# Seven block products for the second feed-forward product, in the slots beside cross-attention

## The chip, the cores and the metric

The kernel runs on one core of one Trainium2 chip. The metric is the device time of one execution in microseconds (us); all data is float32. The engines are called by the names of the profile: PE (TensorE, matrix products), PEld (its weight loads), DVE (VectorE), ACT (ScalarE), POOL (GpSimd) and SP (the queue that issues most transfers here).

## What is computed

The input `x` has 8 batches of 256 tokens with 256 features. It passes through three residual stages, each followed by a layer norm:

```python
x = layernorm(x + attn(x))       # 4 layers: self-attention and an MLP 256 -> 1024 -> 256, exact gelu
x = layernorm(x + xattn(x, ctx)) # cross-attention to 120 context rows, 16 heads of 64
x = layernorm(x + ffn(x))        # W1, W2 composed from 32 low-rank terms each, tanh gelu
```

The last stage is `h = gelu(x @ W1); y = h @ W2` with W1 of 256x1024 and W2 of 1024x256. An MLP of the first stage has the same shapes, with biases. The cross-attention has a mask under which query i sees key j only where j = i (mod 256), so that each query attends to one key of its own or to none.

## The kernel before

All weights and the running `x` of each batch (`xs[b]`, two tiles of 128 tokens by 256 features) stay on the core. The program has no scheduler for PE, ACT, DVE and POOL: their instructions run in the order in which the source issues them (`manual_schedule`), and each engine works through its own queue in that order. SP's order is the framework's.

The 32 units of self-attention (4 layers x 8 batches) run in a first loop, each MLP four units behind its attention. A second loop (lines 1413 to 1460) has 16 slots, of which 11 have work:

- Slots 0 to 7 run the cross-attention of batch `s` (class `Cross`) beside a feed-forward `ff`.
- In slots 0, 1 and 2 `ff` is the last three MLPs of layer 3 (class `Mlp`, batches 5, 6, 7); in slots 3 to 10 it is the composed feed-forward of batches 0 to 7 (class `Composed`). So slots 8, 9 and 10 have a feed-forward alone.

Both feed-forwards are a `Seven`: the first product, transposed (`hT`, 1024 rows by 256 tokens), is a 2x2 by 2x2 block product done with seven block products instead of eight, in Winograd's form. Each block product (`one`, line 596) is four matmuls with 128 moving columns. Its operand sums are made on POOL: those of W1 once for each layer (`first_sums`, lines 560 to 563), those of the turned input for each batch (`turn_sums`, lines 574 to 577). The seven are issued in the groups `p16`, `p5`, `p27` and `p34`, with DVE and ACT adding partial sums between them:

- `p16`: blocks 1 and 6; ACT copies block 1, DVE adds it to block 6 in PSUM (line 614).
- `p5`: block 5; ACT copies the two partial sums (lines 620, 622).
- `p27`: block 2 ends h11, which ACT puts through gelu; block 7, added by DVE to h22 (line 628), then gelu.
- `p34`: block 3, added by DVE to h21 (line 633), then gelu; block 4 ends h12, then gelu.

So the four gelus run on ACT in the order h11, h22, h21, h12. An `Mlp` does each as four activations of 128 columns, with a bias (line 918); a `Composed` as one of 512 (line 960).

The second product before (`second`, line 645) is a plain one: for token tile i, eight matmuls with `hT` blocks as weights and 256 columns of W2 moving. `second(1)` reads h22 and h21, `second(0)` reads h11 and h12. In an MLP both fill one PSUM bank, and DVE adds it to `xs[b]` (line 233). In a composed feed-forward each tile has its own bank; DVE adds it (line 973), normalises that tile (`bn_stats`, lines 181 to 184; a power on POOL, line 189; a scaling on DVE, line 195) and SP writes 128 KB (line 976).

At the end of a slot before, PE's order is: block 4 of `ff`; `turn_o` (transposes of the cross-attention's values); `second(1)`; `nxt_m.turn` (four transposes of the next feed-forward's input, line 214) with `turn_sums` on POOL; `second(0)`; `x.out` (the output projection, lines 1176 to 1179, added by DVE at line 233); `nxt_x.turn` (two transposes, line 1079, then a copy on DVE and two bias additions on POOL, line 229). DVE centres the next batch (`nxt_x.centre`, line 195) between. The next slot begins with the cross-attention's `scores` (line 1090). In a slot `old.finish_moments` and `old.finish` normalise the previous cross-attention's batch on DVE, after `p16`.

The PSUM pool `bank_g`, from which all feed-forward banks come, has four banks.

Of the kernel before, what the change touches and what calls it, by code (L numbers as in the profile page):

```python
# [8 lines left out]
F32 = mybir.dt.float32  # L9
# [6 lines left out]
P = 128  # L16
# [5 lines left out]
def tile_decoder_postln(  # L22
# [29 lines left out]
    nc = tc.nc  # L52

    B, T, D = x.shape
    DEPTH = Wq.shape[0]
    WT = T // P
# [12 lines left out]
    NP, _, R = fc1_A.shape  # L69
# [4 lines left out]
    out_v = out.rearrange("b (w p) d -> p (b w) d", p=P)  # L74
# [8 lines left out]
    xs = [const.tile([P, WT, D], F32, name=f"x_{b}") for b in range(B)]  # L83

    def load_x(b, queue):
        queue.dma_start(out=xs[b], in_=x_v[:, b * WT : (b + 1) * WT, :])
# [16 lines left out]
    at = 0  # L103
    offs = {}
    for name, v in (("g1", ln1_g), ("b1", ln1_b), ("g2", ln2_g), ("b2", ln2_b), ("ff", b1)):
        n = v.shape[0] * v.shape[1] // P
# [18 lines left out]
    w2c = const.tile([P, NF, D], F32, name="w2c")  # L125
# [30 lines left out]
    mlp_ws = {}  # L156
# [5 lines left out]
    work = ctx.enter_context(tc.tile_pool(name="work", bufs=2))  # L162
# [8 lines left out]
    def bank_g(name):  # L171
        return ps_g.tile([P, 512], F32, tag="bank_g", name=name)
# [19 lines left out]
    def centre(dst, src, mv, rstd):  # L192

        for i in range(src.shape[1]):
            nc.vector.tensor_scalar(  # L195
                dst[:, i, :],
                src[:, i, :],
                mv[:, i, 0:1],
                rstd[:, i : i + 1],
                ALU.subtract,  # L200
                ALU.mult,
            )

    def normalise(dst, src, name, last=False):
        centre(dst, src, *moments(src, name, last))
# [447 lines left out]
                        between()  # L653


    class Attention:


# [286 lines left out]
    class Composed(Seven):  # L945
# [24 lines left out]
        def second(self, i):  # L970
            super().second(i)
            x, at = xs[self.b][:, i : i + 1, :], self.b * WT + i
            nc.vector.tensor_add(x[:, 0, :], x[:, 0, :], self.ps[:, i * D : (i + 1) * D])
            y = work.tile([P, 1, D], F32, tag="xnm", name=f"y_{self.name}_{i}")
            normalise(y, x, f"{self.name}_{i}", self.b == B - 1)
            nc.sync.dma_start(out=out_v[:, at : at + 1, :], in_=y)

# [3 lines left out]
    class Context:  # L983
# [29 lines left out]
        def take(self):  # L1013
            b0, ps = self.b0, self.ps
            nc.vector.tensor_copy(
                self.cT[:, :, b0 : b0 + 2, :],
                ps[:, : 2 * NC * S2].rearrange("p (c b j) -> p c b j", c=NC, b=2),
            )
# [39 lines left out]
    class Cross:  # L1058
# [128 lines left out]
        finish = centre  # L1187
# [17 lines left out]
    UNITS = DEPTH * B  # L1205
    compose = Compose()
    cross = None
# [20 lines left out]
        out=before,  # L1228
        in_=before,
# [49 lines left out]
    nxt_x = None  # L1279
    nxt_m = None  # L1280
    nxt_c = None
    mlp_sums = {}
    for s in range(1, UNITS + 1):
        ff = nxt_m
        after = Attention(s + 1) if s + 1 < UNITS else None
        nxt_m = Mlp(s + 1 - LAG) if s + 1 >= LAG else None
        filled = cross is None
        if after and filled and s > 1:
            after.moments()
        if new and s > 1:  # L1290
            new.qkv(nxt_c)
        nxt_c = None
        if filled:
            compose.combine(0)
            if compose.done():
                compose.last.final()
                comp_stack.close()
                cross = ctx.enter_context(tc.tile_pool(name="cross", bufs=1))
        if s == 1:
            compose.run()  # L1300
            after.moments()
        if not new:
            ff.turn()
            ff.turn_sums()
            old.totals()
            old.divide(range(HL))
        old.linear_sums()
        old.divide_c()
        if not new:
            ff.p16()  # L1310
        old.turn_p()
        if ff and new:
            ff.turn()
            ff.turn_sums()
            compose.combine(1)
        if new:
            new.scores()
        old.values()
        if not new:
            nxt_x = Cross(0, cx)  # L1320
            nxt_x.moments()
        if 2 < s + 2 < B:
            load_x(s + 2, nc.scalar)
        if s == 1:
            mlp_ws[0] = load_mlp(0, nc.scalar)
        if after and filled and not ff:
            after.centre()
        if s == 1:
            next(first[1])
            next(first[1])  # L1330
        if ff:
            if new:
                ff.p16()
            if after and filled:
                after.centre()
            elif after:
                after.moments()
            old.out(0)
            ff.p5()
            ff.p27()  # L1340
            old.out(1)
            ff.p34()
            compose.weigh()
        else:
            compose.run()
            old.out(0)
            old.out(1)
            if s == 1:
                for _ in range(3):
                    next(first[1])  # L1350
        if after and not filled:
            after.centre()
        if nxt_m:
            nxt_m.moments()
        if s == LAG - 2:
            mlp_sums[0] = first_sums(mlp_ws[0][0])
        if ff and ff.b == B - 1 and ff.l + 1 < DEPTH:
            mlp_sums[ff.l + 1] = first_sums(mlp_ws[ff.l + 1][0])
        turn_cx = cx and s < UNITS
        if turn_cx:  # L1360
            i = 2 * (s - (UNITS - B + LAG))
            cx.turn(i)
            cx.take()
        if new:
            new.exps()
            if not filled:
                new.head_exps((0, 1))

        vsums = None if new else cx.sums()
        if ff:  # L1370
            ff.second(1, vsums and (lambda: next(vsums)))
        if vsums:
            next(vsums)
        if after:
            after.turn()
        if new:
            new.head_exps((2, 3) if not filled else range(HL))
            new.softmax_q()
        if filled:
            compose.run()  # L1380
        if new and after:
            new.totals()
            new.divide(range(HL))
        if nxt_m and after and not filled:
            nxt_c = nxt_m.centre
        elif nxt_m:
            nxt_m.centre()
        if ff:
            ff.second(0)
        l, b = divmod(s + 1, B)  # L1390
        if b == B - 2 and l + 1 < DEPTH:
            attn_ws[l + 1] = load_attn(l + 1, nc.scalar)
        l, b = divmod(s + 1 - LAG, B)
        if l >= 0 and b == B - 2 and l + 1 < DEPTH:
            mlp_ws[l + 1] = load_mlp(l + 1, nc.scalar)
        if s == UNITS - B + LAG - 1:
            xwq = wpool.tile([P, NC, XI], F32, tag="w1", name="xwq")
            xwo = wpool.tile([P, NM, D], F32, tag="w2", name="xwo")
            cx = Context()
            nc.sync.dma_start(out=xwq, in_=xWq.rearrange("(c p) n -> p c n", p=P))  # L1400
            nc.sync.dma_start(out=xwo, in_=xWout.rearrange("(c p) n -> p c n", p=P))
        if turn_cx:
            cx.take_sums()
            if i == B // 2 - 2:
                cx.load(1)
        if s == UNITS:
            nxt_x.centre()
            cx.project()
        old, new = new, after
    nxt_x.turn()  # L1410
    nxt_m.turn()
    old = None
    for s in range(2 * B):
        x, ff = nxt_x, nxt_m
        nxt_x = Cross(s + 1, cx) if s + 1 < B else None
        u = UNITS - LAG + s + 2
        nxt_m = Mlp(u) if u < UNITS else Composed(u - UNITS) if u < UNITS + B else None
        if ff and s == 0:
            ff.turn_sums()
        if x:  # L1420
            x.scores()
        if ff:
            ff.p16()
        if old:
            old.finish_moments()
        if x:
            x.values(0)
        if old:
            old.finish()
        old = x  # L1430
        if ff:
            ff.p5()
            ff.p27()
        if nxt_x:
            nxt_x.moments()
        if x:
            x.values(1)
        if nxt_m:
            nxt_m.moments()
        if ff:  # L1440
            ff.p34()
        if nxt_m:
            nxt_m.centre()
        if u == UNITS:
            mlp_sums[DEPTH] = first_sums(w1c)
        if x:
            x.turn_o()
        if ff:
            ff.second(1)
        if nxt_m:  # L1450
            nxt_m.turn()
            nxt_m.turn_sums()
        if nxt_x:
            nxt_x.centre()
        if ff:
            ff.second(0)
        if x:
            x.out()
        if nxt_x:
            nxt_x.turn()  # L1460


# [56 lines left out]
```

## Time and profile before

| | us |
|---|---|
| median of three runs | 1214.65 (1214.35 to 1214.76) |
| the profiled execution, its time | 1214.1 |
| the profiled execution, its span | 1212.1 |
| start of slot 0 (first matmul of its scores) | 928.38 |
| start of slot 3 | 1017.00 |
| start of slot 8 | 1164.16 |
| start of the last `second` pair (slot 10) | 1200.07 |

The profile is of one execution. A line of the timeline has the start and the duration in us, the engine, the source line, the operation, what it writes and reads (the program's names), the shapes, and how many instructions were merged (x16); in brackets stands the idle time before it and what ended that. A line with several instructions gives the whole stretch. Matmuls are pipelined and their ends are modelled, so two neighbouring starts say more than a duration.

### The profile page before, as it was taken

The page shows a single profiled execution, that of the slowest core. Times are in us where ns is not written, and L with a number is a line of the kernel's source. Part 1 is how long each engine was busy: PE and PEld are TensorE (multiplying, and loading weights), DVE is VectorE, ACT ScalarE, POOL GpSimd, SP SyncE. Part 2 cuts the span into 40 slices and gives each one's busy share as a digit, 9 for nine tenths or more (in the row PEclk, how much of TensorE's full clock was granted, in tenths as well). Part 3 has the DMA queues.
Part 4 walks back from the last instruction along what each step waited for, and adds up shares of the span by engine and source line. Part 5 has one row for each costly group of instructions (what it writes and reads, how often), then busy time and mean ns, then how long its engine had stood idle before and what let it go on. Part 6 is the DMA issues. An engine that isn't in the chain of part 4 may idle for free.

```text
span 1212.1 us, 24094 instructions
## 1 busy us (share of the span) xinstructions
PE 1198.7 (99%) x9133; PEld 960.7 (79%) x9133; DVE 852.5 (70%) x2422; ACT 636.8 (53%) x1774; POOL 440.0 (36%) x663
## 2 busy tenths in 40 slices
PE   8999999999999999999999999999999999999998
PEld 5556789888888888878888888888787777777787
DVE  6878788777878777677877777777874455555543
ACT  4444555655444567766677666776563333323223
POOL 6665455555565322222422222242232223222220
PEclk9999999999999999999999999999999999999999
DMA  5633131101310120020001002021000000000000
GB/s 161 211 89 113 44 92 45 40 24 30 115 45 1 29 98 2 1 65 12 1 1 41 1 2 75 2 70 26 10 11 9 1 9 10 18 18 9 10 14 23
DMA packets 29505, 47.81 MB, mean 39 GB/s; under 512 B 3150, under 2 KB 22734, under 8 KB 29134
## 3 DMA queue, kind: packets, MB, share of 16 engines
q0 software_dynamic: 6656, 20.98, 5.9%
q10 hardware_dynamic: 13024, 14.07, 3.6%
q1 hardware_dynamic: 9710, 11.23, 2.9%
q8 instruction: 72, 1.18, 0.4%
q14 instruction: 43, 0.35, 0.1%
HBM read 44.17 MB, written 2.10 MB: 38 GB/s over the span
## 4 chain that ended last, share of the span: by engine, by line
PE 96%; DVE 3%; ACT 1%; issue 0%; POOL 0%; POOLq 0%; ACTq 0%; DVEq 0%
PE ps_p_m L645 18%; PE qkv_a L713 9%; PE ps_h_m_u L596 7%; PE ps_h_m_a L596 5%; PE ps_h_m_d L596 5%; PE ps_p_a L239 5%; PE ps_w L387 5%; PE ps_qk_a L693 4%; PE ps_w L449 4%; PE ps_p_f L645 4%; PE ps_pT_a L860 3%; PE sc_a L744 2%; PE ps_y_c L1179 2%; PE ps_xq_c L1090 2%; PE ps_xk_c L1090 2%; PE ps_xv_c L1090 2%
## 5 line engine op out<-in xcount | busy, mean ns | idle before, releaser
L645 PE MATMUL ps_p_m<-w,h_m 128*128 128x256 f32 x1024 | 233.5, 380 | 0.0
L645 PEld LDWEIGHTS ps_p_m<-w,h_m 128*128 128x128 f32 x1024 | 189.4, 191 | 22.8 <-ACT h_m L918 0.3
L229 POOL TENSOR_TENSOR x<-x,b 128x256 f32<-128x256 f32 x64 | 48.3, 774 | 226.2 <-DVE xn_m L195 226.2
L713 PE MATMUL qkv_a<-wa,xT_a 128*128 128x512 f32 x256 | 115.1, 592 | 0.0
L775 ACT ACTIVATE p_a<-sc_a,nm_a 128x128 f32<-128x128 f32 (+1 forms) x256 | 103.6, 430 | 2.2 <-DVE nm_a L757 2.0
L713 PEld LDWEIGHTS qkv_a<-wa,xT_a 128*128 128x128 f32 x256 | 48.7, 190 | 47.5 <-issue 45.8
L757 DVE TENSOR_REDUCE nm_a<-sc_a 128x1 f32<-128x128 f32 (+1 forms) x256 | 79.5, 352 | 4.4
L918 ACT ACTIVATE h_m<-h_m,cols 128x128 f32<-128x128 f32 x256 | 78.6, 405 | 6.2 <-DVE h_m L633 5.5
L229 POOL TENSOR_TENSOR x<-x,bo 128x256 f32<-128x256 f32 x64 | 48.1, 771 | 73.3 <-DVE xn_a L195 73.2
L596 PE MATMUL ps_h_m_a<-xT_m,w 128*128 128x128 f32 x512 | 70.6, 281 | 0.5 <-DVE xT_m L223 0.5
L300 POOL DMA_INDIRECT ga<-in_L_ffn_fc_A_dram,idx_a x64 | 62.2, 972 | 23.6 <-issue 15.3
L720 ACT COPY v<-qkv_a 128x256 f32<-128x256 f32 x64 | 23.8, 372 | 84.5 <-PE qkv_a L713 84.5
L596 PE MATMUL ps_h_m_u<-tx_m,w 128*128 128x128 f32 x512 | 67.8, 276 | 0.0
L596 PEld LDWEIGHTS ps_h_m_a<-xT_m,w 128*128 128x128 f32 x512 | 62.4, 192 | 4.8 <-issue 1.5
L239 PE MATMUL ps_p_a<-wo,oT_a 128*128 128x256 f32 x256 | 65.7, 381 | 0.0
L805 DVE TENSOR_TENSOR p_a<-p_a,psum_a 128x384 f32<-128x384 f32 x128 | 63.8, 560 | 1.1
L596 PEld LDWEIGHTS ps_h_m_u<-tx_m,w 128*128 128x128 f32 x512 | 62.3, 192 | 0.0
L693 PE MATMUL ps_qk_a<-xT_a,wa 128*128 128x256 f32 x256 | 60.7, 380 | 0.9 <-ACT aw L354 0.9
L645 PE MATMUL ps_p_f<-w2c,h_f 128*128 128x256 f32 x256 | 57.8, 380 | 0.0
L387 PE MATMUL ps_w<-gbt,at 128*128 128x512 f32 x128 | 56.7, 596 | 0.0
L753 DVE TENSOR_TENSOR sc_a<-sc_a,causal 128x256 f32<-128x256 f32 x128 | 54.3, 424 | 3.4 <-PE sc_a L744 2.2
L775 ACT ACTIVATION_READ_ACCUMULATOR p_a<-sc_a,nm_a 128x1 f32 x256 | 55.8, 218 | 0.0
(269 smaller groups left out, 2704.0 us busy)
## 6 DMA issues: line engine op xcount, KB each, us to landing
w<-in_L_attn_W_dram ACTq DMA_DIRECT2D x8, 1024.0 KB, 6.3
xwkv<-in_L_xattn_Wkv_dram SPq DMA_DIRECT2D x1, 2048.0 KB, 9.1
x_c<-in_x_dram SPq DMA_DIRECT2D x8, 256.0 KB, 2.6
out_dram<-y_f SPq DMA_DIRECT2D x16, 128.0 KB, 1.7
x<-in_x_dram ACTq DMA_DIRECT2D x6, 256.0 KB, 3.4
ga<-in_L_ffn_fc_A_dram,idx_a POOLq DMA_INDIRECT x64, 3.4
xwq<-in_L_xattn_Wq_dram SPq DMA_DIRECT2D x1, 1024.0 KB, 5.1
xwo<-in_L_xattn_Wout_dram SPq DMA_DIRECT2D x1, 1024.0 KB
```

What stands on the lines that cost most here:

```text
L229: nc.gpsimd.tensor_add(xb[:, i, :], xb[:, i, :], bias)
L239: nc.tensor.matmul(ps[:, i * D : (i + 1) * D], lhs(c, i), w[:, c, :], start=c == 0, stop=c == n_in - 1,)
L387: nc.tensor.matmul(ps, self.at[k][:, m * P : (m + 1) * P], self.b[k][:, n * 512 : (n + 1) * 512], start=k == 0, stop=k == PG - 1,)
L596: nc.tensor.matmul(ps[:, f * P : (f + 1) * P], self.ws[n][:, f * P : (f + 1) * P], self.rhs[n], start=start and f == 0, stop=stop and f == ...
L645: nc.tensor.matmul(self.ps[:, i * D : (i + 1) * D], self.h[k][:, f, :], self.w2[:, half * 4 + f, :], start=k in (11, 22) and f == 0, stop= ...
L693: nc.tensor.matmul(ps[s], wa[:, c, s * HW : (s + 1) * HW], xT[:, c, :], start=c == 0, stop=c == NC - 1,)
L713: nc.tensor.matmul(t, xT[:, c, w * P : (w + 1) * P], wa[:, c, 2 * HW :], start=c == 0, stop=c == NC - 1,)
L757: nc.vector.tensor_reduce(self.nmax[:, h, w : w + 1], sc[:, s], AX.X, ALU.max, negate=True)
L775: nc.scalar.activation(flat[:, s], sc[:, s], AF.Exp, bias=self.nmax[:, h, w : w + 1], accum_out=self.psum[:, h, w : w + 1],)
L805: nc.vector.tensor_tensor(p, p, self.psum[:, h, :, None].to_broadcast([P, 3, P]), ALU.mult)
L918: nc.scalar.activation(dst[:, f, :], src[:, f * P : (f + 1) * P], AF.Gelu, bias=col("ff", i))
L1090: nc.tensor.matmul(ps[:S2], lhs(c), w[:, c, off : off + 512], start=c == 0, stop=c == NC - 1)
```

## The change

In the eight slots with cross-attention the second product is done with seven block products too, and the end of the slot has a new order. Slots 8 to 10 keep the old form.

New functions (in `Seven`, and `w2_sums` beside it):

```diff
+        def two(self, n, ps, slot, a, start=False):
+            for f in range(4):
+                nc.tensor.matmul(
+                    ps[:, slot * P : (slot + 1) * P],
+                    a[:, f, :],
+                    self.w2s[n][:, f, :],
+                    start=start and f == 0,
+                    stop=f == 3,
+                    skip_group_check=True,
+                )
+        def take(self, blocks, src):
+            x = xs[self.b].rearrange("p i (n d) -> p (i n) d", n=2)[:, blocks, :]
+            nc.vector.tensor_add(x, x, src)
+        def second_plain(self):
+            h = self.h
+            self.ps = bank_g(f"ps_p_{self.name}")
+            self.two(1, self.ps, 0, h[11], start=True)
+            self.two(4, self.ps, 2, h[22])
+            self.two(2, self.ps, 1, h[12])
+        def h_sums(self):
+            h = self.h
+            s1, s2 = (cross.tile([P, 4, P], F32, tag=f"h{i}", name=f"h{i}_{self.name}") for i in (1, 2))
+            nc.gpsimd.tensor_add(s1, h[21], h[22])
+            nc.gpsimd.tensor_sub(s2, s1, h[11])
+            nc.gpsimd.tensor_sub(h[21], h[11], h[21])
+            nc.gpsimd.tensor_sub(h[22], h[12], s2)
+            self.hs = {5: s1, 6: s2, 7: h[21], 3: h[22]}
+        def second_early(self):
+            ps = self.ps.rearrange("p (k d) -> p k d", k=4)
+            self.take(slice(0, 1), ps[:, 0:1, :])
+            self.take(slice(0, 3, 2), ps[:, 1:3, :])
+        def second_sums(self):
+            ps, hs = self.ps, self.hs
+            pd = bank_g(f"ps_pd_{self.name}")
+            self.two(6, ps, 0, hs[6])
+            self.take(slice(1, 2), ps[:, None, :P])
+            self.two(5, pd, 0, hs[5], start=True)
+            self.take(slice(3, 4), pd[:, None, :P])
+            self.two(7, ps, 0, hs[7])
+            self.take(slice(2, 4), ps[:, None, :P].to_broadcast([P, 2, P]))
+            self.two(3, pd, 0, hs[3])
+            self.take(slice(1, 2), pd[:, None, :P])
+    def w2_sums(w2):
...
+        nc.gpsimd.tensor_sub(t1, b[0][1], b[0][0])
+        nc.gpsimd.tensor_sub(t2, b[1][1], t1)
+        nc.gpsimd.tensor_sub(t3, b[1][1], b[0][1])
+        nc.gpsimd.tensor_sub(t4, b[1][0], t2)
```

`two` is one block product: four matmuls with 128 moving columns. Blocks 1, 4 and 2 use plain blocks of h (with sums of W2 only in block 4); blocks 6, 5, 7 and 3 use sums of h, which POOL makes in `h_sums`. Blocks 6 and 7 add up in the PSUM columns that hold block 1, and `take` adds the columns to the 128x128 blocks of `xs[b]` that they belong to. `w2_sums` makes the sums of W2: once before slot 0 for the MLP's, and once at the end of slot 2 for the composed W2.

The end of a slot and the composed feed-forward's last step:

```diff
         if s == UNITS:
             nxt_x.centre()
             cx.project()
+            w2s = w2_sums(mlp_ws[DEPTH - 1][1])
...
         if x:
             x.turn_o()
-        if ff:
-            ff.second(1)
-        if nxt_m:
+            ff.w2s = w2s
+            ff.second_plain()
+            ff.h_sums()
             nxt_m.turn()
             nxt_m.turn_sums()
-        if nxt_x:
-            nxt_x.centre()
-        if ff:
+            ff.second_early()
+            if nxt_x:
+                nxt_x.centre()
+            x.out()
+            if nxt_x:
+                nxt_x.turn()
+            ff.second_sums()
+            if u == UNITS:
+                w2s = w2_sums(w2c)
+            if u > UNITS:
+                ff.finish()
+        elif ff:
+            ff.second(1)
+            if nxt_m:
+                nxt_m.turn()
+                nxt_m.turn_sums()
             ff.second(0)
-        if x:
-            x.out()
-        if nxt_x:
-            nxt_x.turn()
...
+        def finish(self):
+            at = self.b * WT
+            y = work.tile([P, WT, D], F32, tag="xnm", name=f"y_{self.name}")
+            normalise(y, xs[self.b], self.name)
+            nc.sync.dma_start(out=out_v[:, at : at + WT, :], in_=y)
```

PE's order at the end of a slot becomes: `turn_o`; blocks 1, 4, 2; the next feed-forward's transposes; `x.out`; the next cross-attention's transposes; blocks 6, 5, 7, 3. On DVE the order is: the copy of `nxt_m.turn`, two takes, `nxt_x.centre`, `x.out`'s addition, the copy of `nxt_x.turn`, four takes, and in slots 3 to 7 `finish`, which normalises both tiles of the batch at once. On POOL `h_sums` stands ahead of `turn_sums`, and the composed `w2_sums` behind the bias additions of slot 2. Two output writes of 128 KB become one of 256 KB in each of the slots 3 to 7.

More of the change, by code (lines that the diff above doesn't have):

```diff
@@ new lines, in w2_sums @@
+    def w2_sums(w2):
+        b = [[w2[:, 4 * k : 4 * k + 4, n * P : (n + 1) * P] for n in range(2)] for k in range(2)]
+        t1, t2, t3, t4 = (cross.tile([P, 4, P], F32, tag=f"t{i}", name=f"t{i}") for i in range(1, 5))
+        nc.gpsimd.tensor_sub(t1, b[0][1], b[0][0])
+        nc.gpsimd.tensor_sub(t2, b[1][1], t1)
+        nc.gpsimd.tensor_sub(t3, b[1][1], b[0][1])
+        nc.gpsimd.tensor_sub(t4, b[1][0], t2)
+        return {1: b[0][0], 2: b[1][0], 3: b[1][1], 4: t4, 5: t1, 6: t2, 7: t3}
```

## The prediction

> **What bounds the kernel now.** First the head of the page with its chain of waits, which say which engine sets the end:
>
> ```profile
> span 1212.1 us, 24094 instructions
> PE 1198.7 (99%) x9133; PEld 960.7 (79%) x9133; DVE 852.5 (70%) x2422; ACT 636.8 (53%) x1774; POOL 440.0 (36%) x663
> PE 96%; DVE 3%; ACT 1%; issue 0%; POOL 0%; POOLq 0%; ACTq 0%; DVEq 0%
> ```
>
> TensorE is busy 99% of the span and is 96% of the chain: a matmul step saved is time saved, unless a new wait on TensorE eats it. Second, the timeline of TensorE in one of the eight slots with cross-attention, at the first composed feed-forward (slot 3):
>
> ```profile
> 1032.65 1.06 PE L596 MATMUL ps_h_f_u<-tx_f,w1c 128*128 128x128 f32 x8
> 1033.54 0.38 PE L1152 MATMUL ps_sh_c<-ident,xsh_c 128*128 128x128 f32 x2
> 1033.76 0.99 PE L1161 MATMUL ps_xoT_c<-ident,xo_c 120*128 120x120 f32 x8
> 1034.58 3.63 PE L645 MATMUL ps_p_f<-w2c,h_f 128*128 128x256 f32 x16
> 1038.04 0.60 PE L214 MATMUL ps_t_f<-ident,x 128*128 128x128 f32 x4
> 1038.48 3.62 PE L645 MATMUL ps_p_f<-w2c,h_f 128*128 128x256 f32 x16
> 1041.93 0.60 PE L1176 MATMUL ps_y_c<-vproj,shT_c 128*128 128x256 f32 x2
> ```
>
> The ends are modelled, so I read starts. Each matmul of the source is two steps (8 calls give x16). Sixteen 256-wide steps take 1038.04 - 1034.58 = 3.46 us, 0.216 a step; eight 128-wide ones 1033.54 - 1032.65 = 0.89, 0.112 a step. There is no gap. Third, what feeds the end of the first product in slot 1, an Mlp slot, on TensorE, ACT and DVE:
>
> ```profile
> 975.45 3.81 PE L645 MATMUL ps_p_m<-w,h_m 128*128 128x256 f32 x16
> 979.09 0.60 PE L214 MATMUL ps_t_m<-ident,xn_m 128*128 128x128 f32 x4
> 976.81 1.28 ACT L918 ACTIVATE h_m<-h_m,cols 128x128 f32<-128x128 f32 x4 [2.47 <-DVE h_m L633]
> 977.99 1.11 ACT L918 ACTIVATE h_m<-ps_h_m_u,cols 128x128 f32<-128x128 f32 x4
> 978.99 0.56 ACT L1171 COPY xoT<-ps_xoT_c 128x480 f32<-128x480 f32 x1
> ```
>
> h12, the last gelu, is ready only at 979.10. The old order read it last, after 22, 21, four transposes and 11, so this was hidden; even so this slot's first half took 3.64 instead of 3.46, because h21's first quarter (0.4 after 976.81) came late: wake-up about 0.16. Fourth, slot 8, the first without cross-attention:
>
> ```profile
> 1166.21 0.70 DVE L614 TENSOR_TENSOR ps_h_f_u<-ps_h_f_u,h_f 128x512 f32<-128x512 f32 x1 [1.17 <-PE ps_h_f_u L596]
> 1166.82 0.42 DVE L181 BATCH_NORM_STATS2 st_c_n<-x 128x6 f32<-128x256 f32 x1
> 1168.26 0.70 POOL L189 TENSOR_TENSOR rs_c_n<-rs_c_n,neghalf 128x2 f32<-128x2 f32 x1 [6.31 <-DVE rs_c_n L184]
> 1168.99 0.74 DVE L195 TENSOR_SCALAR x<-x,mv_c_n,rs_c_n 128x256 f32<-128x256 f32 x2 [0.81 <-POOL rs_c_n L189]
> 1169.64 0.68 DVE L628 TENSOR_TENSOR h_f<-h_f,ps_h_f_u 128x512 f32<-128x512 f32 x1
> 1170.47 1.13 PE L596 MATMUL ps_h_f_u<-tx_f,w1c 128*128 128x128 f32 x8 [0.77 <-DVE h_f L628]
> ```
>
> Here DVE is on the path: TensorE waits for h22's sum, which stands behind a normalisation of 1169.64 - 1166.82 = 2.82 us.
>
> **The matmuls.** Per slot, 32 steps of 256 go (2 x 3.46 = 6.92) and 7 x 8 = 56 steps of 128 come (7 x 0.893 = 6.25): -0.667, in 8 slots -5.34. The nearest rows for a 128-wide step with its own weights are the first products (0.89 in every block), so I take no other price.
>
> **h12 is read earlier.** It is now the third block product, 16 steps or 1.785 us after the start. A gelu is four quarters, each awaited by itself; in the row of 1.11 they end at 0.405, 0.64, 0.875 and 1.11. With 0.16 for the wake-up, slot 1 has the last quarter at 979.10 + 0.16 + 0.223 = 979.48, against 975.45 + 2.678 = 978.13 without waiting: +1.35, and the old 0.18 (for h21, no longer read here) goes: +1.17. Slot 0 starts at 945.97 with that gelu row at 947.35: last quarter 948.46, done 948.84 against 948.65: +0.20. Slot 2 (1005.11, gelu row 1006.35 to 1007.46): +0.06. In composed slots h12 is one gelu, in slot 3 at 1035.20 for 0.58; needed at 1034.58 + 1.785 = 1036.37: hidden with 0.4 left. Sum +1.43. Behind the waiting matmul are four transposes and x.out; ScalarE's copy of xoT (978.99) is done before x.out's fifth projection.
>
> **GpSimd's sums.** h_sums is four 128x512 operations; nearest rows 1.27 to 1.36 (lines 560 to 563), so about 5.2 a slot, ahead of turn_sums in GpSimd's queue. They start with h21 (1035.29 in slot 3) and M6's sum is there after two, 1037.9; TensorE arrives after 2.68 + 0.43 + 4.32 + 0.22 = 7.65 us, at 1042.2. Slot 2 is tightest: first_sums (line 563, 1008.63 for 1.27) runs first, s2 is ready at about 1012.5, wanted at 1012.82. turn_sums ends near 1017 there, wanted at 1024. w2_sums before slot 0 takes 5.2 from 926.05; bias and the second turn sum end near 933.6, wanted at 936.14. The second w2_sums ends near 1023.5; the memsets behind it are wanted by DVE near 1026. All at nothing; without cover, each lost microsecond is one on TensorE.
>
> **The takes.** Six adds from PSUM replace one or two. 128x128 from PSUM: the nearest row is 0.29 (line 726), bounds 0.17 (120x16 rows) and 0.69 (512 wide). Let T be the start of nxt_x.turn. x.out's add and the xT copy hold DVE to T + 1.23; block 6 ends at T + 1.28, its take at T + 1.6; TensorE wants that slot at T + 2.0: 0.24 left after the wake-up. At 0.69 it would be about 0.16 a slot, 1.3 in all. I take 0, since width decides in all DVE rows.
>
> **finish.** In slots 3 to 7 one normalisation of both tiles and one 256 KB write replace two; SP issues five fewer. The normalisation moves to the head of the next slot. In slots 4 to 7 that is hidden: DVE is free by 3.33 us after the head, and the next work, xk times xq, comes at 3.7. In slot 8 it is not. With S the start of its first matmul: last take to S + 0.48, normalisation 2.82, so u's add starts at S + 3.33 (before S + 2.05). ScalarE's copy of u ends at 4.64; block 7 starts at 4.8 instead of 3.57; cross 7's normalisation follows (another 2.82), h22's add is S + 6.76 to 7.44, block 4 starts at 7.59 instead of 1170.47 - 1164.16 = 6.31: +1.28.
>
> **Sum.** -5.34 + 1.43 + 1.28 = **-2.63**: span 1209.5. The profiled execution took 1214.1, 2.0 over its span, and the median is 1214.65; taking 2.6 from the median gives **1212.0 us**. Bounds: -5.3 if none of the stalls appears (1209.3), +1.3 if the takes cost their upper bound (1213.3).
>
> **Rivals.**
> *The waits don't come* (chance 0.12): DVE or ScalarE work drifts and h12 comes in time, or slot 8 absorbs finish: one or both of the 1.2 us terms go, 1209.3 to 1211. Against it: slot 1's lateness comes from DVE's statistics ahead of h21 (L633 at 976.09), which the change does not touch.
> *Given back* (0.13): takes at their upper bound, slot 2's GpSimd margin gone: 1213.2 to 1216. For it: margins of 0.24 and 0.3. Against: no DVE row is that long at this width.
> *DVE arrives late at T* (0.07, slower): GpSimd now runs beside DVE's centring of nxt_x. In the timeline two such centrings took 1.67 beside GpSimd's 128x512 add (1029.89) and 0.74 without (1168.99). If DVE came over 0.24 late to block 6's take, block 7 waits. One microsecond late is 0.76 a slot, 6.1 in all: 1218. Against: DVE ends centring about 1 us before T even at 1.67. The Trainium skill (SBUF — State Buffer, Who interferes with whom) says that DVE and GpSimd share a port pair that one holds exclusively for an instruction; that trace agrees, and by the same section an add with one operand in PSUM is free of it.
> *A narrow step is held by its weight load* (0.02): the load rows have a mean of 191 ns. At that 56 steps cost 10.7 a slot, +3.8, in eight +30: 1245. Against: 128-wide first products already run at 112 ns with as many loads. The Trainium skill (TensorE: Matmul & The Clock Gate, Back-to-back issue gap) speaks for this rival: it has sustained streams at about 81 ns for 128 columns and 131 for 512, so halving the width would save far less than half; the trace disagrees, 112 against 216 for 256.
>
> **How the numbers follow.** The forecast holds 0.66, from 1211.2 to 1213.1. 0.2% is 2.4 us, about what a measurement of this kernel can tell from no change: below 1212.2 is faster, above 1217.1 slower. About two thirds of the forecast (0.43) and the first rival (0.12) are faster, 0.55; the rest of it with the second rival 0.36; slower 0.09. The range 1210.2 to 1214.4 takes the forecast and half of the first two rivals, 0.8.
>
> **What would show it.** Eight 128-wide steps of the new products 0.89 apart; slots 3 to 6 at 28.8 us instead of 29.48 (1046.47 to 1075.95); TensorE waiting for ScalarE's h12 over 1 us in slot 1, little in 0 and 2; block 7 and block 4 of slot 8 late, its length 14.62 before and 15.9 after. Wrong if TensorE waits on GpSimd or DVE in second_sums, or if slots 3 to 6 are not shorter by 0.67.

## The result, and the profile after

| | before | after |
|---|---|---|
| median of 19 runs each, us | 1214.56 | 1212.01 |
| ratio of the runs | | 0.9979 (0.9972 to 0.9985) |
| profiled execution, its time and its span | 1214.1, 1212.1 | 1212.26, 1210.5 |

The change saves 2.55 us, against 2.6 predicted (1212.0). That is 0.21%, just past the 0.2% that the prediction took as the bound of what can be told; the interval reaches to both sides of it. It allows a saving of 1.8 to 3.4 us, so that the agreement to 0.1 us is finer than these runs can tell; what bears the forecast out is the slots.

Slot lengths, from the start of a slot's first matmul (TensorE's timeline) to that of the next, show where the time came from:

| slot | before | after | predicted |
|---|---|---|---|
| 0 | 29.48 | 29.01 | 29.01 |
| 1 | 29.66 | 30.16 | 30.16 |
| 2 | 29.48 | 28.89 | 28.87 |
| 3 to 6 | 29.47 to 29.48 | 28.82 | 28.8 |
| 7 | 29.26 | 28.60 | 28.59 |
| 8 | 14.62 | 15.92 | 15.9 |
| 9 | 14.32 | 14.33 | as before |

The predicted column is the length before with the prediction's terms of that slot added. The ten differences add up to 262.19 - 264.72 = -2.53 us. In this one profile slot 0 also starts 0.65 later than before (929.03 against 928.38), and from the start of slot 10 to the end of the span it is 0.3 longer (19.3 against 19.0), so its span fell by 1.6 only. The 0.65 comes ahead of anything that the change adds. It is there, to 0.03, at TensorE's first product of the first attention (`ps_qk_a`, 8.95 against 8.33), behind the 28 matmul steps on the identity (`ps_idle`) that open the program. In the old kernel's profile these start 0.21 us apart and pass to 0.11 after some twenty of them; in the new one's all are 0.21 apart, so that they take 6.13 instead of 5.46. In the profiles of the six experiments on the first two chips `ps_qk_a` starts between 8.05 and 8.98, and in all eight profiles the projection of the values, which precedes slot 0, follows 915.9 to 916.1 later. What sets the moment of that step stays open.

The head of the page and the chain of waits, after:

```profile
span 1210.5 us, 24572 instructions
PE 1194.7 (99%) x9325; PEld 962.7 (80%) x9325; DVE 867.1 (72%) x2452; ACT 637.4 (53%) x1774; POOL 488.6 (40%) x698
PE 94%; DVE 4%; ACT 1%; issue 1%; POOL 0%; POOLq 0%; ACTq 0%; DVEq 0%
```

TensorE has 192 matmul steps more and is busy 4 us less. GpSimd has 48.6 us more, and none of the added sums is in the chain. DVE's share grew in two places: in slot 1, where the chain now leaves TensorE at 965.08 and comes back to it only at block 2, at 978.56, with 9.3 us of DVE in between where there were none, and in slot 8, with 4.9 us of DVE instead of 3.0.

TensorE's timeline in slot 3, after:

```profile
1034.67 1.06 PE L661 MATMUL ps_p_f<-w2c,h_f 128*128 128x128 f32 x8
1035.57 1.06 PE L661 MATMUL ps_p_f<-t,h_f 128*128 128x128 f32 x8
1036.47 1.06 PE L661 MATMUL ps_p_f<-w2c,h_f 128*128 128x128 f32 x8
1037.36 0.60 PE L214 MATMUL ps_t_f<-ident,x 128*128 128x128 f32 x4
...
1044.12 1.06 PE L661 MATMUL ps_p_f<-t,h_f 128*128 128x128 f32 x8
1045.01 1.06 PE L661 MATMUL ps_pd_f<-w2c,h_f 128*128 128x128 f32 x8
1045.91 1.02 PE L1159 MATMUL ps_xk_c<-xwkv,cT 128*120 128x512 f32 x2
```

Every block product takes 0.89 or 0.90 to the next start, as the first product's do, and no row has a bracket: no wait at all in this slot.

Slot 1 has the wait that the prediction priced. First TensorE, then ACT:

```profile
975.63 1.06 PE L661 MATMUL ps_p_m<-w,h_m 128*128 128x128 f32 x8
976.53 1.06 PE L661 MATMUL ps_p_m<-t,h_m 128*128 128x128 f32 x8
978.56 1.25 PE L661 MATMUL ps_p_m<-w,h_m 128*128 128x128 f32 x8 [0.98 <-ACT h_m L981]
979.65 0.60 PE L214 MATMUL ps_t_m<-ident,xn_m 128*128 128x128 f32 x4
```

```profile
976.98 1.28 ACT L981 ACTIVATE h_m<-h_m,cols 128x128 f32<-128x128 f32 x4 [2.46 <-DVE h_m L633]
978.16 1.11 ACT L981 ACTIVATE h_m<-ps_h_m_u,cols 128x128 f32<-128x128 f32 x4
```

ACT begins h12's four gelus at 978.16, the first ends 0.35 later, and block 2 starts at 978.56. The bracket shows 0.98; the whole price is larger, since each later pair of steps waits for its own quarter (1.09 instead of 0.89 to the next start): 979.65 instead of 975.63 + 3 x 0.893 = 978.31, so 1.34.

Slot 8, DVE, ACT and TensorE together:

```profile
1164.33 0.69 DVE L614 TENSOR_TENSOR ps_h_f_u<-ps_h_f_u,h_f 128x512 f32<-128x512 f32 x1
1164.93 0.42 DVE L181 BATCH_NORM_STATS2 st_c_n<-x 128x6 f32<-128x256 f32 x1
1165.11 0.59 ACT L620 COPY h_f<-ps_h_f_u 128x512 f32<-128x512 f32 x1 [2.47 <-DVE ps_h_f_u L614]
...
1165.84 1.13 PE L596 MATMUL ps_h_f_u<-tx_f,w1c 128*128 128x128 f32 x8 [1.14 <-ACT h_f L620]
...
1167.75 0.68 DVE L628 TENSOR_TENSOR h_f<-h_f,ps_h_f_u 128x512 f32<-128x512 f32 x1
...
1168.58 1.13 PE L596 MATMUL ps_h_f_u<-tx_f,w1c 128*128 128x128 f32 x8 [0.71 <-DVE h_f L628]
```

The slot starts at 1160.97. The sum for u (L614) comes at +3.36, block 7 at +4.87 and block 4 at +7.61; predicted were +3.33, +4.8 and +7.59. The brackets name ACT for the first wait, but ACT had itself waited 2.47 for DVE: the cause is the normalisation of slot 7's batch in front of L614.

GpSimd in slot 2, the tightest:

```profile
1010.55 1.32 POOL L686 TENSOR_TENSOR h_m<-h_m,h_m 128x512 f32<-128x512 f32 x1
1011.95 1.27 POOL L687 TENSOR_TENSOR h_m<-h_m,h_m 128x512 f32<-128x512 f32 x1
```

The sum for block 6 is ready at 1013.22, and block 6 starts at 1013.51: 0.29 left.

### The profile page after: what moved, and what is told of

Read it like the earlier page. It is cut to its first block, busy times and chain, and to the rows that moved or that the text cites. A ratio compares the mean times of both kernels' runs of the same rounds, so it can differ in the third digit from the quotient of the medians.

```text
span 1210.5 us, 24572 instructions
## 1 busy us (share of the span) xinstructions
PE 1194.7 (99%) x9325; PEld 962.7 (80%) x9325; DVE 867.1 (72%) x2452; ACT 637.4 (53%) x1774; POOL 488.6 (40%) x698
## 4 chain that ended last, share of the span: by engine, by line
PE 94%; DVE 4%; ACT 1%; issue 1%; POOL 0%; POOLq 0%; ACTq 0%; DVEq 0%
PE ps_p_m L645 17%; PE qkv_a L776 9%; PE ps_h_m_u L596 7%; PE ps_h_m_a L596 5%; PE ps_p_a L239 5%; PE ps_w L387 5%; PE ps_h_m_d L596 5%; PE ps_qk_a L756 4%; PE ps_w L449 4%; PE ps_pT_a L923 3%; PE sc_a L807 2%; PE ps_y_c L1248 2%; PE ps_xq_c L1159 2%; PE ps_xk_c L1159 2%; PE ps_ao_a L939 2%; PE ps_xv_c L1159 2%
## 5 line engine op out<-in xcount | busy, mean ns | idle before, releaser
L645 PE MATMUL ps_p_m<-w,h_m 128*128 128x256 f32 x928 | 211.6, 380 | 0.0
L645 PEld LDWEIGHTS ps_p_m<-w,h_m 128*128 128x128 f32 x928 | 171.4, 190 | 20.6
L776 PEld LDWEIGHTS qkv_a<-wa,xT_a 128*128 128x128 f32 x256 | 48.6, 190 | 47.6 <-issue 45.9
L189 POOL TENSOR_TENSOR rs_a<-rs_a,neghalf 128x2 f32<-128x2 f32 x32 | 22.8, 712 | 81.2 <-DVE rs_a L184 81.2
```

The lines of the kernel that those rows point to most:

```text
L645: nc.tensor.matmul(self.ps[:, i * D : (i + 1) * D], self.h[k][:, f, :], self.w2[:, half * 4 + f, :], start=k in (11, 22) and f == 0, stop= ...
L776: nc.tensor.matmul(t, xT[:, c, w * P : (w + 1) * P], wa[:, c, 2 * HW :], start=c == 0, stop=c == NC - 1,)
```

## The experiments

The theory is that of the prediction: the block products save 0.66 a slot, h12's earlier reading (slots 0 to 2) gives back 1.4 and the joint `finish` in slot 8 gives back 1.3, and the work on GpSimd and DVE is hidden, with small margins. The rivals are that a wait removed comes back at the next late operation, that the new order and not the products brings the gain, and that the hidden work isn't hidden. Six kernels shared chips on which the kernel before had medians of 1214.45 and 1214.48; the last two (e7, e8) ran on one where the kernel before took 1227.1 and slot 0 starts some 12 us later, so those go by ratio and by slot. Slots are compared with after's, above.

### Block 2 moved behind x.out (e1_m2_late)

```diff
             self.two(4, self.ps, 2, h[22])
-            self.two(2, self.ps, 1, h[12])
+        def second_late(self):
+            self.two(2, self.ps, 1, self.h[12])
...
-            self.take(slice(0, 1), ps[:, 0:1, :])
-            self.take(slice(0, 3, 2), ps[:, 1:3, :])
+            self.take(slice(0, 3, 2), ps[:, 0:3:2, :])
...
             self.take(slice(2, 4), ps[:, None, :P].to_broadcast([P, 2, P]))
+            self.take(slice(0, 1), ps[:, None, P : 2 * P])
...
             x.out()
+            ff.second_late()
```

> Block 2 (the one that reads h12) is issued behind the output projection, everything else as in the changed kernel. Theory (the product's gain is partly returned by the wait for h12): the waits of slots 0, 1 and 2 go, 0.19 + 1.34 + 0.07 = 1.6 us by the changed kernel's timeline; slot 1 shrinks from 30.16 to 28.8 us; time about 1210.4. Rival (TensorE then meets the next late thing, a take or a sum on GpSimd): the wait comes back in the same slots and the time stays near 1212.0.

Measured: 1210.95 us, ratio 0.9974 (0.9962 to 0.9985). Slots 0 and 2 are 28.82; slot 1 is 29.35, 0.53 over. TensorE in slot 1 of this kernel, then DVE:

```profile
976.08 1.06 PE L661 MATMUL ps_p_m<-t,h_m 128*128 128x128 f32 x8
977.19 0.87 PE L214 MATMUL ps_t_m<-ident,xn_m 128*128 128x128 f32 x4
977.90 0.65 PE L1247 MATMUL ps_y_c<-vproj,shT_c 128*128 128x256 f32 x2
```

```profile
975.83 0.68 DVE L633 TENSOR_TENSOR h_m<-h_m,ps_h_m_d 128x512 f32<-128x512 f32 x1
976.73 0.74 DVE L195 TENSOR_SCALAR xn_m<-x,mv_m,rs_m 128x256 f32<-128x256 f32 x2 [0.22 <-POOL rs_m L189]
977.38 0.42 DVE L1227 COPY shT_c<-ps_sh_c 128x256 f32<-128x256 f32 x1
```

The wait for ACT is gone. What follows was late too: the transposes' input xn_m is centred on DVE at 976.73, so the four transposes start at 977.19 instead of 976.97 and take 0.71 to the next start instead of 0.44; the copy of shT_c then holds x.out by the few hundredths that are left. So the 1.4 is right as what h12 costs in this change, but it had covered 0.5 of DVE's lateness in slot 1: there the rival is right for 0.5 of the 1.34 and the theory for the rest, and in slots 0 and 2 the theory is.

### The last finish moved into slot 8, behind p34 (e2_finish_late)

```diff
-            if u > UNITS:
+            if u > UNITS and nxt_x:
                 ff.finish()
+            elif u > UNITS:
+                late = ff
...
         if ff:
             ff.p34()
+        if late:
+            late.finish()
+            late = None
```

> The normalisation of the last batch beside cross-attention moves from the end of slot 7 to behind the first product of slot 8. Theory (it holds up DVE at the head of slot 8): slot 8 goes from 15.92 back to about 14.6 us, time about 1210.7. Rival (slot 8 is held by the cross-attention's normalisation alone, which was there before): slot 8 stays near 15.9 and the time near 1212.0.

Measured: 1210.52 us, ratio 0.9968 (0.9956 to 0.998). Slot 8 is 14.64. The two matmuls that had waited:

```profile
1164.17 1.13 PE L596 MATMUL ps_h_f_u<-tx_f,w1c 128*128 128x128 f32 x8
...
1166.92 1.13 PE L596 MATMUL ps_h_f_u<-tx_f,w1c 128*128 128x128 f32 x8 [0.73 <-DVE h_f L628]
```

With the slot's start at 1160.60 block 7 is back at +3.57 and block 4 at +6.32; what block 4 still waits for is cross-attention 7's normalisation, as before the change. The prediction's term is confirmed.

### Both, and cross-attention 7's normalisation behind p34 too (e3_both_later)

The two edits above, with slot 7's finish moved on to slot 10, and:

```diff
-        if old:
+        if old and x:
             old.finish_moments()
...
-        if old:
+        if old and x:
             old.finish()
-        old = x
+        last, old = old if not x else None, x
...
         if ff:
             ff.p34()
+        if last:
+            last.finish_moments()
+            last.finish()
+        if late and not nxt_m:
+            late.finish()
+            late = None
```

> Block 2 late as in the first run; the normalisation of the batch of slot 7 moves to slot 10, and that of the last cross-attention batch behind the first product of slot 8. Theory (the terms add): 1.6 us from h12, and slot 8 as long as slot 9, 14.3 us instead of 15.92: in all 3.2 us below the changed kernel, about 1208.8, 5.7 below the kernel before. Rival (what is moved collides with slot 9 or the end): slot 9 or the tail gets longer by one to three us, 1210 to 1212.

Measured: 1209.07 us, ratio 0.9955 (0.9941 to 0.9968): faster than both kernels, 2.9 us below after, whose ratio of 0.9979 (0.9972 to 0.9985) lies outside this interval. Slot 8 is 13.96, slot 9 14.33:

```profile
1163.27 1.13 PE L596 MATMUL ps_h_f_u<-tx_f,w1c 128*128 128x128 f32 x8
...
1164.51 0.69 DVE L628 TENSOR_TENSOR h_f<-h_f,ps_h_f_u 128x512 f32<-128x512 f32 x1 [2.06 <-PE ps_h_f_u L596]
...
1165.35 1.13 PE L596 MATMUL ps_h_f_u<-tx_f,w1c 128*128 128x128 f32 x8
```

Here DVE waits for TensorE (2.06 ahead of L628), and neither block 7 nor block 4 has a bracket. The 0.66 that slot 8 already lost in the kernel before (14.62 against 13.96) is gone as well.

### Plain second product in the new order (e5_plain_new_order)

```diff
-            ff.second_plain()
-            ff.h_sums()
+            Seven.second(ff, 1)
...
-            ff.second_early()
+            if isinstance(ff, Composed):
+                ff.add_tile(1)
...
-            ff.second_sums()
-            if u == UNITS:
-                w2s = w2_sums(w2c)
+            Seven.second(ff, 0)
+            if isinstance(ff, Composed):
+                ff.add_tile(0)
+            else:
+                add_to(xs[ff.b], ff.ps)
```

`w2_sums` is gone with it; the order of the slot and the one `finish` stay.

> The order of the changed kernel with the plain second product: tile 1 (h22, h21) in the place of blocks 1, 4, 2 and tile 0 (h11, h12) in the place of blocks 6, 5, 7, 3; one normalisation of both tiles at the end of the slot; no sums on GpSimd. Theory (the gain is the matmuls' alone): slots 3 to 6 are 29.48 us as before, no wait for h12, slot 8 near 15.9; time about 1.3 above the kernel before, 1215.9. Rival (part of the gain comes from the order, or from one normalisation and one write in place of two): slots 3 to 6 shorter than 29.48, time at or below 1214.5.

Measured: 1216.12 us, ratio 1.0013 (1.0004 to 1.0023). Slots 0 to 6 are those of the kernel before (29.48, 29.66, 29.48 and so on); slot 8 is 16.06, 1.44 over. So the order and `finish` alone cost what was expected, and all the gain is the products': in slots 3 to 6 the two kernels differ by 0.66 each.

### The first two sums of h made twice (e4_pool_twice) and the first alone made twice (e7_pool_one)

```diff
             nc.gpsimd.tensor_add(s1, h[21], h[22])
             nc.gpsimd.tensor_sub(s2, s1, h[11])
+            nc.gpsimd.tensor_add(s1, h[21], h[22])
+            nc.gpsimd.tensor_sub(s2, s1, h[11])
```

> GpSimd makes the first two sums of h twice in each of the eight slots: 2 x 1.3 us more in its queue ahead of block 6. Theory (GpSimd is hidden by about 3 us, but in slot 2 by 0.3): only slot 2 waits, about 2.4 us, on block 6; time about 1214.4. Rival (GpSimd is on the path): 2.6 us in every slot, 20 us in all. Rival (it is hidden everywhere): no change, 1212.0.

Measured: 1216.08 us, ratio 1.0013 (1.0004 to 1.0023). In the profiled execution only slot 2 changed, but it is 33.05, 4.2 over 28.89, where the wait alone had been expected. TensorE there, and the windows of the same stretch (their columns: length, busy time of PE, PEld, DVE, ACT and POOL, granted clock, DMA share, GB/s):

```profile
1015.69 1.35 PE L661 MATMUL ps_p_m<-t,h_m 128*128 128x128 f32 x8 [2.27 <-POOL h_m L689]
1016.84 1.92 PE L661 MATMUL ps_pd_m<-t,h_m 128*128 128x128 f32 x8
1018.54 1.72 PE L661 MATMUL ps_p_m<-t,h_m 128*128 128x128 f32 x8
1020.10 1.06 PE L661 MATMUL ps_pd_m<-w,h_m 128*128 128x128 f32 x8
```

```profile
1008.00:1013.30 5.30, 5.30 (x30) 4.62 (x29) 2.85 (x6) 0.73 (x2) 5.14 (x5) 1.00 0.02 3
...
1015.70:1016.90 1.20, 1.20 (x9) 1.20 (x10) 0.00 (x0) 0.00 (x0) 1.20 (x2) 0.84 0.00 0
1016.90:1018.50 1.60, 1.60 (x9) 1.60 (x9) 0.29 (x1) 0.00 (x0) 1.60 (x2) 0.50 0.00 0
1018.50:1020.10 1.60, 1.60 (x10) 1.60 (x9) 0.29 (x1) 0.00 (x0) 1.52 (x5) 0.55 0.00 0
```

The wait is as expected: block 6 starts at 1015.69 on GpSimd's second h sum. Then blocks 6, 5 and 7 take 1.15, 1.70 and 1.56 instead of 0.89, in all 1.74 more, and the granted clock of just that stretch is 0.84, 0.50 and 0.55. It doesn't come in every execution: of the ten runs three took 1214.77 to 1214.90 us at a mean granted clock of 1.00, about what the wait alone gives (1212.0 + 2.4), and the other seven 1216.02 to 1217.88 at 0.997 to 0.999. It could be the idle time that brought the clock down, or GpSimd working beside. To tell these apart, e7 makes the first sum alone twice:

```diff
-            nc.gpsimd.tensor_add(s1, h[21], h[22])
+            for _ in range(2):
+                nc.gpsimd.tensor_add(s1, h[21], h[22])
```

> Asked: with block 6's sum twice late, TensorE waited 2.27 us in slot 2 and then ran three block products at about half speed (1.70 and 1.56 us instead of 0.89), with a granted clock of 0.50 to 0.55 there. Was that the idle time, or GpSimd working beside? Here only the first sum (h21 + h22) is made twice, a redundant 1.27 us; GpSimd is busy through the whole stretch again. Theory (the long idle time brought it): block 6 of slot 2 waits for GpSimd 1.27 - 0.29 = about 1.0 us, the products behind it run 0.89 each at clock 1.00, slot 2 is 28.89 + 1.0 = 29.9 us, all other slots as they are; 1213.0 us. Rival (GpSimd beside TensorE, or reading sums just made): the products behind block 6 are slow here too, by the same 1.7 us in all; slot 2 is 31.6, 1214.7 us.

Measured: ratio 0.9984 (0.9974 to 0.9993) to the kernel before on that chip. Slot 2 is 30.11, 1.22 over; the others are after's to 0.01.

```profile
1027.03 1.16 PE L661 MATMUL ps_p_m<-t,h_m 128*128 128x128 f32 x8 [0.96 <-POOL h_m L688]
1028.03 1.06 PE L661 MATMUL ps_pd_m<-t,h_m 128*128 128x128 f32 x8
1028.92 1.06 PE L661 MATMUL ps_p_m<-t,h_m 128*128 128x128 f32 x8
```

```profile
1027.03:1028.10 1.07, 1.07 (x9) 1.07 (x10) 0.00 (x0) 0.00 (x0) 1.07 (x1) 1.00 0.00 0
1028.10:1030.00 1.90, 1.90 (x19) 1.90 (x19) 0.57 (x2) 0.00 (x0) 1.82 (x4) 1.00 0.00 0
```

GpSimd is busy throughout here too, and the products behind block 6 take 0.89 at clock 1.00. What settles it stands in the first 100 us of the same trace. TensorE waits there 2.44 us for ACT, and later once 2.63, in work that the change doesn't touch, and behind each wait come stretches at half the clock. In the two below GpSimd (the fifth busy time) has 0.11 us of work, and none:

```profile
33.53 1.18 PE L369 MATMUL ps_at<-ident,aw 128*128 128x128 f32 x4 [2.44 <-ACT w2c L405]
```

```profile
37.00:40.00 3.00, 3.00 (x24) 2.07 (x22) 1.38 (x6) 1.40 (x4) 0.11 (x1) 0.50 0.39 153
98.20:101.60 3.40, 3.40 (x50) 2.18 (x43) 3.26 (x11) 1.57 (x5) 0.00 (x0) 0.50 0.08 13
```

The same four matmuls take 0.60 in after, which doesn't wait there. So GpSimd beside TensorE neither suffices for the lower clock (slot 2 here) nor is needed for it (the first 100 us), and what the cases have in common is the long idle time. The margin in slot 2 is 0.29 as read. The redundant sum puts 1.35 more ahead of block 6's sum (1.27, and 0.08 before it), so that this sum comes 1.06 late. Block 6 then starts 1.12 later in its slot than in after, and its first steps add 0.10 (1.00 to the next start instead of 0.89).

### DVE late at the takes (e6_dve_late, e8_dve_later)

```diff
-            nc.vector.tensor_copy(self.xT.rearrange("p c i -> p (c i)"), pt[:, :D])
+            for _ in range(2):
+                nc.vector.tensor_copy(self.xT.rearrange("p c i -> p (c i)"), pt[:, :D])
```

e8 has the same with `range(3)`. The copies beyond the first are redundant, as are the sums made again in e4 and e7.

> DVE copies the next cross-attention's turned input twice, which makes it about 0.43 us late for the take of block 6 in slots 0 to 6. Theory (that take has about 0.24 us left before block 7 waits): block 7 waits 0.2 us in each of the seven slots, 1.4 in all, time about 1213.4. Rival (DVE has no room at all there): 0.43 in each, 3.0 in all, 1215. Rival (DVE is off the path): no change, 1212.0.

Measured: 1212.68 us, ratio 0.9985 (0.9975 to 0.9994). Each of slots 0 to 6 is 0.08 to 0.09 longer than after's, 0.6 in all; 1.4 was expected.

```profile
1043.96 0.28 DVE L673 TENSOR_TENSOR x<-x,ps_p_f 128x128 f32<-128x128 f32 x1
1044.38 1.13 PE L661 MATMUL ps_p_f<-t,h_f 128*128 128x128 f32 x8
```

Block 6's take ends at 1044.24 and block 7 starts at 1044.38, 0.02 later than its place at 1043.47 + 0.89, so the margin is just used up here. The other 0.08 is block 7's first steps, 0.97 to the next start. It was smaller than expected because the take in after waits 0.1 for block 6 in any case, so that the second copy delays it by less than its length. That leaves two readings, a true threshold or lateness that is absorbed, which e8 separates:

> The copy of nxt_x.turn is made three times, so that DVE comes to block 6's take another 0.38 us or so later than with two. Theory (with two copies the margin was just used up, and from there each late microsecond on DVE is TensorE's at block 7, in every slot): slots 0 to 6 are each about 28.90 + 0.38 = 29.28 us, block 7 waits for DVE about 0.45; 1212.68 + 7 x 0.38 = 1215.3 us, slower than before. Rival (DVE's lateness is mostly absorbed by its short takes and by idle time between them, as the 0.09 a slot with two copies might mean): slots 28.9 to 29.0, 1212.7 to 1213.3 us.

Measured: ratio 1.0004 (0.9995 to 1.0014) on the chip of e7, so the whole gain is lost. Slots 0 to 6 are 207.39 in all, against 203.34 in after: 0.58 a slot, and 0.49 more than with two copies.

```profile
1057.64 0.28 DVE L673 TENSOR_TENSOR x<-x,ps_p_f 128x128 f32<-128x128 f32 x1
1057.84 0.28 DVE L673 TENSOR_TENSOR x<-x,ps_pd_f 128x128 f32<-128x128 f32 x1
```

```profile
1058.06 1.13 PE L661 MATMUL ps_p_f<-t,h_f 128*128 128x128 f32 x8 [0.31 <-DVE x L673]
```

Block 6's take ends at 1057.92, block 7 starts 0.14 later, and nothing is absorbed: from the threshold on, DVE's time is TensorE's. The expectation of 0.38 a slot beyond e6 was a little low, since the third copy adds about 0.45 to the row (1.33 for three, 0.88 for two). Six of the slots have 0.46 more than with two copies. Slot 5 has another 0.2: TensorE's transposes of the values wait there for DVE's `xo_c`, which ends 0.26 later against them than in slot 4; why, stays open.

## Why the prediction was right

- **The matmuls**, -0.667 a slot: measured -0.65 or -0.66 in slots 3 to 7, so -5.2 in eight against -5.34. e5 shows that nothing else in the change brings a gain.
- **h12 read earlier**, +1.43: slot 0 0.19 (predicted 0.20), slot 1 1.16 net (1.17), slot 2 0.07 (0.06). What made it exact was to count from the last of the four gelus and not from the first, and to put 0.16 on it; in the trace of slot 1 these are 0.12 until TensorE starts and 0.03 in that step itself, and behind the first gelu TensorE starts after 0.05.
- **finish**, +1.28: 1.30 in slot 8, with block 7 and block 4 each at their predicted place to 0.07. In slots 4 to 7 it was hidden: in slot 4 of after DVE is done with it at 1049.35, and the next work it must not delay starts at 1049.61.
- **GpSimd's sums**, nothing: 1.27 to 1.33 each, and 0.29 left in slot 2 where 0.3 was predicted; e7 shows that the margin is that, and what it costs past it.
- **The takes**, nothing: 0.28 to 0.29 for 128x128, as the nearest row had it. The margin predicted for block 7 was 0.24; e6 used it up with one 0.42 copy and e8 shows the full price behind it. The prediction priced a late take in all eight slots; slot 7 turns no further input, and it stays at 28.60 in both, so its upper bound and its rival "DVE late at T" should have counted seven.
- **The rivals.** "The waits don't come": they came, all three. "Given back": neither the takes nor GpSimd made TensorE wait in any slot. "A narrow step is held by its weight load": eight steps take 0.89 wherever nothing is awaited. "DVE late at T": its trigger was there, since DVE's centring of `nxt_x` beside GpSimd rose to 1.72 to 1.85 us; but as the prediction had it, DVE was done in time, in slot 3 1.6 ahead of x.out's addition:

```profile
1038.99 1.74 DVE L195 TENSOR_SCALAR x<-x,mv_c,rs_c 128x256 f32<-128x256 f32 x2
1042.32 0.69 DVE L233 TENSOR_TENSOR x<-x,ps_y_c 128x512 f32<-128x512 f32 x1 [1.59 <-PE ps_y_c L1248]
```

Two limits of it showed only in the experiments. The prediction wrote each lost microsecond of GpSimd's cover as one on TensorE; for the first that held (in e7 1.06 us of lateness cost 1.22), but in e4 2.4 us of it cost 4.2 in the profiled execution, since the clock came down. And e1 was expected to get back the 1.6 us of all the waits for h12 (the 1.4 is net of an older wait that the change removes); it got 1.07 by slots (0.19, 0.81 and 0.07), because the next input in slot 1 was late as well.

## What to carry to other kernels

When a matmul product is cut into narrower block products, price the saving by steps and widths from rows of the same kernel, then look at each input by the time at which its last piece is ready: here more than half of the saving of 5.2 us went to one gelu read earlier and one normalisation put ahead of a bounding addition, and both could be moved out of the way (e3, another 2.9 us with an older wait of slot 8). Work that is hidden by a few tenths of a microsecond is worth measuring by doing it twice: it gives the margin, and the slope behind it.

## What the runs showed that was not expected

A single idle time of TensorE of 2.3 to 2.6 us was enough to bring its clock down. In the profile of e4 the wait of 2.27 us was followed by about 3.4 us at half the clock (worked out from 0.84, 0.50 and 0.55 in the windows above, so it began some 0.8 us after TensorE had started again), which cost 1.74 on top of the wait. The first 100 us of e7 and e8 hold four more cases, with waits of 2.44 and 2.63 us and of 2.48 and 2.54. With up to 1.38 us (a wait for DVE at about 906 us in before and after) nothing of the kind follows in any of the ten profiles. The limit lies between 1.38 and 2.27 us in the cases seen; where, these runs don't tell, and the three of e4's runs that kept the clock suggest that 2.27 is not enough each time. The Trainium skill (TensorE: Matmul & The Clock Gate, HAM oscillation — how this bites in real kernels) has the abstract rule as no idle gaps over about 3.4 us; here shorter ones were enough, and the measurement decides.
